# A two-layer model on one core: the first four rows' experts get blocks of their own, the last rows are routed beside them, and the state space's first fronts run beside the other blocks

## The chip, the cores and the metric

The kernel runs on one core of a Trainium2 chip. The core has TensorE (PE, matmuls; PEld is its weight load), VectorE (DVE), ScalarE (ACT), GpSimd (POOL) and SyncE (SP), a queue of DMA instructions for some of them, 16 DMA engines, and PSUM in eight banks of 128 x 512 float32. The time is device microseconds of one launch, the median of several runs. Everything is float32.

## The reference

The input x has 32 rows of 256 tokens of 128 numbers. There are two layers, each an attention-like part and a feed-forward part, and each part is wrapped in the same modulation, whose vectors come from one small matmul per layer:

```python
mod = (_silu(L0_c) @ L0_wmod).reshape(L0_c.shape[0], 6, 1, -1)
h = _layernorm(x, axis=-1) * (1 + ca) + sa
x = x + ga * _L0_attn_ref(h, ...)        # 16 heads of 8, rotary, softmax over 256 keys
h = _layernorm(x, axis=-1) * (1 + cb) + sb
x = x + gb * _L0_ffn_ref(h, ...)         # 8 experts, two per token
```

The feed-forward part of layer 0 gives every token its two best of eight experts:

```python
logits = x @ gate_w
mult, sel = _sparse_mixer_routing(logits)
w = jnp.sum(mult[:, :, None] * (sel[:, :, None] == jnp.arange(E)[None, None, :]), axis=1)
h = jax.nn.silu(jnp.einsum('th,ehf->etf', x, w1)) * jnp.einsum('th,ehf->etf', x, w3)
out = jnp.einsum('etf,efh,te->th', h, w2, w)
```

with 512 hidden units. Layer 1 replaces the attention by a Mamba-like state space in both directions (256 channels of 16 states, a scan over the 256 tokens) followed by a Fourier layer, and its experts take one expert per token with a capacity of 80. Only the path of layer 0's experts and the beginning of layer 1's state space matter here.

## The kernel before

**Attention (layer 0).** The order of the instructions is written out by hand. A loop runs over units `s`, eight to a row; a unit computes the scores of two heads of a row, `ex` (L572) and `q` (L576), with the weighted sums `weighted` beside them. Other work is cut into Python generators ("steps", each up to the next `yield`) and put between units: `prepared` (the next row's norm, rotary and projections), `turned` (transposes), `finished` (the output matmul L632, then y and x on POOL, L644 and L646).

**Routing.** `routed(first, n_rows, bank, apart)` (L314) takes a chunk of rows through its norm, gate logits, top two experts and the position of each token among the rows of its expert. `CHUNKS` cuts the 32 rows into six chunks of four and four chunks of two. A list `behind` holds the chunks under way; one step of the oldest is made per unit, two when more than one chunk is in it or in the last row. The last steps of a chunk are the scatters: per tile of 128 tokens two indirect DMAs on POOL's queue (`scattered`, L280; 16 for a chunk of four rows, 8 for one of two) write each token's row, with its destination and its multiplier, into the table `rows_in` in DRAM, in the expert's region. A counter `filled` (one number per expert) says how many rows an expert has so far. Before the first scatter the table has to be blank: `blanked` writes it in four DMAs of 8320 KB on ACT's queue in the units of rows 2 to 5.

**The joint.** The attention loop ends when all streams and `behind` are empty. Then rows 30 and 31 are routed (L781) with the instructions ordered by the compiler's own scheduler, which also schedules everything up to the state space. From `filled` VectorE computes the block table (L785 to L822): for each of `n_blocks` blocks which expert it belongs to, which rows it gathers (`at_u`) and which weights (`w_u`, which is set out of range where the buffer already holds that expert).

**Blocks.** `n_blocks` is 2 x 8192 / 256 + 8 - 1 = 71, since each expert's last block may be partly empty. A block (loop from L826) gathers its weights w (786,432 B, three buffers, L830) and 256 rows h (five buffers, L839) by indirect DMAs on POOL's queue, takes the destinations `to_u` out of h on VectorE (L847), transposes h on TensorE into the bank `ps_m` (L850, two buffers), copies hT (L852), multiplies by w1 and w3 (`pa`, `pb`, L861), gates with Silu on ACT (L862) and a product on VectorE (L863), multiplies by w2 (`po`, L869), scales on ACT (`o`, L877) and scatters the two halves into `rows_out` (L280). `weights_kept` (called at block 17) loads the state space's weights and computes from them `taps` (four POOL multiplies, L700), `spread_a`, `skip` and others.

**State space (layer 1).** Ordered by hand again: a loop over `g`, 16 units to a row, 512 in all, each with `arg` and `ub` matmuls (L1269), an exponential `da` (L1275), a product (L1286) and the scan (L1293) on VectorE, and a product with C on POOL (L1306). A row's unit can begin only when its `front` is done (L1005 to L1111): it adds the two expert outputs from `rows_out` to x, norms it twice, makes the in-projection, the convolution as matmuls, Silu, the x-projection, and dt and u through an exponential and a logarithm. A front is 22 steps, at the places `FRONT_AT` relative to the row's first unit, from -39 to -3.5; `gate` is one step at -9.5. For rows 0, 1 and 2 the loop starts at g = -39, so these steps have no units of another row beside them. A function `table` puts the loads of ACT's function tables where they are needed.

Of the kernel before, what the change touches and what calls it, by code (L numbers as in the profile page):

```python
# [69 lines left out]
def body(ctx: ExitStack, tc: tile.TileContext, a: dict, out: bass.AP):  # L70
# [155 lines left out]
    n_blocks = 2 * n_tok // BR + E - 1  # L226
# [11 lines left out]
    rows_out = scratch.tile([2 * n_tok, D], F32, tag="rows_out", name="rows_out")  # L238
    FILL = 16
    blank = rc.tile([P, FILL, WID], F32, tag="blank", name="blank")  # L240

    def blanked(part, parts):

        if part == 0:
            nc.gpsimd.memset(blank[:], 0.0)
            nc.gpsimd.memset(blank[:, :, D : D + 1], float(4 * n_tok))
        n = room // P // FILL // parts
        flat = rows_in[0:room, :].rearrange("(p a k) w -> p a (k w)", p=P, k=FILL)
        ins = nc.scalar.dma_start(
            flat[:, part * n : (part + 1) * n, :],  # L250
            blank[:].rearrange("p k w -> p (k w)").unsqueeze(1).to_broadcast([P, n, FILL * WID]),
        )
        blanks.append(ins.ins.name)
        if part == 0:
            nc.scalar.dma_start(rows_in[room:, :].rearrange("(p k) w -> p k w", k=2), blank[:, 0:2, :])
# [5 lines left out]
    nc.gpsimd.tensor_scalar(ids2[:], ids[:], float(n_tok), None, ALU.add)  # L261

    filled = rc.tile([P, E], F32, tag="filled", name="filled")
    nc.gpsimd.iota(
        filled[:], pattern=[[n_tok, E]], base=-1, channel_multiplier=0, allow_small_or_imprecise_dtypes=True
    )

    groups = {"in": [], "out": []}  # L270
    sync = mybir.DependencyInfo(mybir.DependencyClass.Sync, mybir.DependencyReason.DATA)
    blanks = []
# [3 lines left out]
    def scattered(group, apart=False, **args):  # L276

        if apart:
            nc.gpsimd.memset(spacer[:], 0.0)
        ins = nc.gpsimd.indirect_dma_start(in_offset=None, **args).ins  # L280
        tc.declare_no_dep(ins, group=group, reason="rows of their own")
        tc.add_to_no_dep_group(group, ins)
        for b in blanks if group == "in" else ():
            tc.add_manual_dep(ins, b, sync, reason="blank rows first")
        groups[group].append(ins.name)

    def reads(group, ins):
        for name in groups[group]:
            tc.add_manual_dep(ins.ins, name, sync, reason="scattered rows")

# [23 lines left out]
    def routed(first, n_rows, bank, apart):  # L314

        n = 2 * n_rows
        k = f"{n}_"
# [78 lines left out]
        for t in range(n):  # L396
            for row_u, h in zip(rows_at, hs):
                scattered(
                    "in",
                    apart,  # L400
                    out=rows_in[:],
# [4 lines left out]


    with ExitStack() as st:
# [8 lines left out]
        def a_bank():  # L417
            return ps_m.tile([P, 512], F32, tag="m", name="m")

# [231 lines left out]
        with tc.manual_schedule(engines=MANUAL):  # L651
            for s in range(-2 * UNITS_A - PREPARED, n_s + 9 * UNITS_A):
# [18 lines left out]
                if i == 2 and b - 2 in range(4):  # L671
                    blanked(b - 2, 4)
                last = b >= n_b - 1
                if i == (0 if last else 2) and b - 1 in starts[1:-1]:
                    c = starts.index(b - 1) - 1
                    behind.append(routed(starts[c], CHUNKS[c], a_bank, True))
                streams[:] = [w for w in streams if next(w, w) is not w]

                for _ in range(2 if last or len(behind) > 1 else 1):
                    if behind and next(behind[0], behind) is behind:  # L680
                        behind.pop(0)
                if s > n_s + UNITS_A + 1 and not streams and not behind:
# [7 lines left out]
    def weights_kept():  # L690
# [50 lines left out]


        das = [wc.tile([P, 4 * T + 1], F32, tag=f"da{i}", name=f"da{i}") for i in range(3)]
        for t in das:
            nc.gpsimd.memset(t[:, :: T], 0.0)

        behind = wc.tile([4 * DS, 1], F32, tag="behind", name="behind")
        nc.vector.tensor_copy(behind[:], ident[: 4 * DS, DTR : DTR + 1])
# [11 lines left out]


    with ExitStack() as st:
# [3 lines left out]
        ps_m = pool(st, "b_psm", 2, PSUM)  # L766
# [3 lines left out]
        iota_p = bc.tile([P, 1], F32, tag="iota_p", name="iota_p")  # L770
        nc.gpsimd.iota(iota_p[:], pattern=[[0, 1]], base=0, channel_multiplier=1, allow_small_or_imprecise_dtypes=True)
        iota_k = bc.tile([P, n_blocks], F32, tag="iota_k", name="iota_k")
        nc.gpsimd.iota(
            iota_k[:], pattern=[[1, n_blocks]], base=0, channel_multiplier=0, allow_small_or_imprecise_dtypes=True
        )
        empty = bc.tile([P, E], F32, tag="empty", name="empty")
        nc.gpsimd.iota(
            empty[:], pattern=[[n_tok, E]], base=-1, channel_multiplier=0, allow_small_or_imprecise_dtypes=True
        )

        for _ in routed(starts[-2], CHUNKS[-1], lambda: ps_m.tile([P, 512], F32, tag="m", name="m"), False):  # L781
            pass


        restart("k")  # L785
        blocks = thin(bc, E)
        nc.vector.tensor_tensor(blocks[:], filled[:], empty[:], ALU.subtract)
        nc.vector.tensor_scalar(blocks[:], blocks[:], 1.0 / BR, 0.5 - 0.5 / BR, ALU.mult, ALU.add)
        nc.vector.tensor_scalar(blocks[:], blocks[:], ROUND, None, ALU.add)
        nc.vector.tensor_scalar(blocks[:], blocks[:], -ROUND, None, ALU.add)  # L790
        upto = thin(bc, E)
        nc.vector.tensor_tensor_scan(upto[:], ones[:, :E], blocks[:], 0.0, ALU.mult, ALU.add)
        past = wide(bc, n_blocks)
        nc.vector.tensor_tensor(
            past[:],
            iota_k[:].unsqueeze(2).to_broadcast([P, n_blocks, E]),
            upto[:].unsqueeze(1).to_broadcast([P, n_blocks, E]),
            ALU.is_ge,
        )
        of = thin(bc, n_blocks)  # L800
        nc.vector.tensor_reduce(of[:], past[:], AX.X, ALU.add)
        nc.vector.tensor_tensor(past[:], past[:], blocks[:].unsqueeze(1).to_broadcast([P, n_blocks, E]), ALU.mult)
        at = thin(bc, n_blocks)
        nc.vector.tensor_reduce(at[:], past[:], AX.X, ALU.add)
        nc.vector.tensor_tensor(at[:], iota_k[:], at[:], ALU.subtract)
        nc.vector.tensor_scalar(at[:], at[:], float(P), None, ALU.mult)

        nc.vector.scalar_tensor_tensor(at[:], of[:], float(n_tok // 2), at[:], ALU.mult, ALU.add)
        nc.vector.tensor_scalar(at[:], at[:], float(room // 2), iota_p[:], ALU.min, ALU.add)
        at_u = bc.tile([P, n_blocks], U32, tag="at_u", name="at_u")  # L810
        nc.vector.tensor_copy(at_u[:], at[:])

        nc.vector.tensor_scalar(of[:], of[:], float(E - 1), float(P), ALU.min, ALU.mult)
        w_at = thin(bc, n_blocks)
        nc.vector.tensor_scalar(w_at[:], of[:], iota_p[:], None, ALU.add)
        same = thin(bc, n_blocks)
        nc.vector.tensor_tensor(same[:, WBUF:], of[:, WBUF:], of[:, : n_blocks - WBUF], ALU.is_equal)
        nc.vector.scalar_tensor_tensor(
            w_at[:, WBUF:], same[:, WBUF:], float(2 * E * P), w_at[:, WBUF:], ALU.mult, ALU.add
        )  # L820
        w_u = bc.tile([P, n_blocks], U32, tag="w_u", name="w_u")
        nc.vector.tensor_copy(w_u[:], w_at[:])  # L822

# [767 lines left out]
```

## Time and profile before

| what | us |
| --- | --- |
| median of the time | 3707.0 (3702.08 to 3708.46, three runs) |
| the profiled execution | 3705.42 |
| its span | 3703.6 |
| attention's last units | 840 to 862 |
| last scatter of rows 30 and 31 | 913.85 |
| first block's first pa | 924.77 |
| last po ends | 1334.9 |
| first arg of the state space | 1390.60 |
| first scan | 1396.33 |

The span is the profiled program from its first to its last instruction; the profiled execution's own time lies 1.8 us above it. "Busy" counts what an engine computes; POOL's time between two indirect DMAs is idle in these rows. A line of a timeline gives start, duration, engine, line, operation, output and inputs, and in brackets how long the engine was idle before and what released it. "PEclk" is the clock that TensorE was granted, as a share of full speed. The granted clock of the whole run was 0.897.

### The profile page before, as it was taken

The page shows a single profiled execution, that of the slowest core. Times are in us where ns is not written, and L with a number is a line of the kernel's source. Part 1 is how long each engine was busy: PE and PEld are TensorE (multiplying, and loading weights), DVE is VectorE, ACT ScalarE, POOL GpSimd, SP SyncE. Part 2 cuts the span into 40 slices and gives each one's busy share as a digit, 9 for nine tenths or more (in the row PEclk, how much of TensorE's full clock was granted, in tenths as well). Part 3 has the DMA queues.
Part 4 walks back from the last instruction along what each step waited for, and adds up shares of the span by engine and source line. Part 5 has one row for each costly group of instructions (what it writes and reads, how often), then busy time and mean ns, then how long its engine had stood idle before and what let it go on. Part 6 is the DMA issues. An engine that isn't in the chain of part 4 may idle for free. (4 is left out here: it accounts for less than half of the span.)

```text
span 3703.6 us, 69018 instructions
## 1 busy us (share of the span) xinstructions
PE 3147.8 (85%) x27464; PEld 2152.1 (58%) x27464; DVE 2612.1 (71%) x3526; ACT 2174.3 (59%) x3286; POOL 2683.4 (72%) x2724
## 2 busy tenths in 40 slices
PE   6988988883999968888889889889889889888864
PEld 3655655552888855555555555556556556555543
DVE  3566666653333318988888898888898888898952
ACT  2666666651333335667676676676676676577661
POOL 4465655555677747888888798888798887798852
PEclk6999999995999989898988898998898898899976
DMA  2630000002233311112112111111111111111112
GB/s 80 271 134 25 25 24 23 26 27 68 82 98 98 97 33 34 29 26 45 32 31 39 32 30 41 32 33 37 32 32 40 32 38 33 32 33 33 24 24 74
DMA packets 149688, 183.29 MB, mean 49 GB/s; under 512 B 31263, under 2 KB 112950, under 8 KB 145140
## 3 DMA queue, kind: packets, MB, share of 16 engines
q1 hardware_dynamic: 121892, 97.72, 11.6%
q0 software_dynamic: 23168, 46.93, 4.0%
q10 hardware_dynamic: 4304, 34.21, 2.2%
q8 instruction: 216, 3.54, 0.4%
q14 instruction: 108, 0.88, 0.1%
HBM read 130.24 MB, written 86.41 MB: 58 GB/s over the span
## 5 line engine op out<-in xcount | busy, mean ns | idle before, releaser
L1306 POOL TENSOR_TENSOR hs<-hs,bc 128x1024 f32<-128x1024 f32 x512 | 1207.0, 2367 | 302.2 <-DVE hs L1293 294.4
L1293 DVE TENSOR_TENSOR_SCAN hs<-da,ub 128x1024 f32<-128x1024 f32 x512 | 1166.1, 2277 | 30.9 <-DVE ub L1286 0.5
L1275 ACT ACTIVATE da<-arg 128x1020 f32<-128x1020 f32 x512 | 522.0, 1019 | 467.4 <-PE ub L1269 374.0
L1269 PE MATMUL arg<-dt,spread_a 32*128 32x256 f32 x4096 | 742.2, 434 | 40.2 <-ACT da L1275 39.2
L1269 PE MATMUL ub<-u,spread 32*128 32x256 f32 x4096 | 649.1, 437 | 88.3 <-POOL u L1111 46.6
L1286 DVE TENSOR_TENSOR ub<-ub,bc 128x1024 f32<-128x1024 f32 x512 | 620.7, 1212 | 40.8 <-PE ub L1269 40.5
L1269 PEld LDWEIGHTS arg<-dt,spread_a 32*128 32x128 f32 x4096 | 442.4, 200 | 201.8 <-ACT da L1275 84.0
L576 DVE TENSOR_REDUCE q<-x 128x4 f32<-128x1024 f32 x256 | 312.8, 1222 | 238.5 <-PE x L569 238.4
L1269 PEld LDWEIGHTS ub<-u,spread 32*128 32x128 f32 x4096 | 393.3, 203 | 143.3 <-DVE hs L1293 71.3
L572 ACT ACTIVATE ex<-e 128x1024 f32<-128x1024 f32 x256 | 262.1, 1024 | 204.6 <-PE x L569 193.5
L569 PE MATMUL e<-qmT,kqT 32*128 32x256 f32 x2048 | 340.9, 415 | 41.2 <-ACT ex L572 41.0
L1325 PE MATMUL y<-hs,gather 128*32 128x256 f32 x4096 | 344.5, 445 | 11.4 <-POOL hs L1306 11.3
L569 PE MATMUL x<-kqT 32*128 32x256 f32 x2048 | 306.8, 417 | 9.2 <-DVE q L576 9.2
L569 PEld LDWEIGHTS e<-qmT,kqT 32*128 32x128 f32 x2048 | 215.9, 191 | 100.2 <-ACT ex L572 72.6
L1053 PE MATMUL m<-oT,taps 128*128 128x256 f32 (+3 forms) x1024 | 264.0, 402 | 3.4 <-ACT xc L1056 2.0
L1180 PE MATMUL m<-coef,mag 128*128 128x128 f32 x1024 | 232.9, 313 | 38.8 <-DVE h L1188 29.1
L1053 PEld LDWEIGHTS m<-oT,taps 128*128 128x128 f32 x1024 | 190.2, 196 | 72.2 <-issue 37.9
L1325 PEld LDWEIGHTS y<-hs,gather 128*32 128x32 f32 x4096 | 123.9, 121 | 183.4 <-issue 98.4
L1180 PEld LDWEIGHTS m<-coef,mag 128*128 128x128 f32 x1024 | 173.8, 213 | 95.1 <-DVE h L1188 41.4
L1180 PE MATMUL m<-coef,r 128*128 128x128 f32 x1024 | 214.3, 294 | 0.0
L280 POOL DMA_INDIRECT rows_out<-o,to_u x142 | 144.5, 1018 | 87.5 <-ACT o L877 65.7
L569 PEld LDWEIGHTS x<-kqT 32*128 32x128 f32 x2048 | 187.6, 192 | 23.2 <-DVE q L576 19.8
(332 smaller groups left out, 6082.9 us busy)
## 6 DMA issues: line engine op xcount, KB each, us to landing
rows_in<-blank ACTq DMA_DIRECT2D x4, 8320.0 KB, 25.4
bc_d<-xd SPq DMA_DIRECT2D x64, 256.0 KB, 5.3
bc<-bc_d SPq DMA_DIRECT2D x32, 512.0 KB, 3.7
of_two<-rows_out SPq DMA_DIRECT2D x64, 128.0 KB, 2.6
mod_b<-mod SPq DMA_DIRECT2D x32, 256.0 KB, 4.0
mod<-mod SPq DMA_DIRECT2D x32, 192.0 KB, 3.1
x<-in_x SPq DMA_DIRECT2D x16, 256.0 KB, 5.3
mod<-mod SPq DMA_DIRECT2D x32, 128.0 KB, 3.0
```

Source lines behind the costliest of these rows:

```text
L280: ins = nc.gpsimd.indirect_dma_start(in_offset=None, **args).ins
L569: nc.tensor.matmul(to, lhs, rhs, start=True, stop=True)
L572: nc.scalar.activation(ex[:], exs[k_e][:], AF.Exp, scale=1.0 / math.sqrt(DH))
L576: nc.vector.tensor_reduce(pad("q", b)[:, :, 2 * i : 2 * i + 2, DH].rearrange("p t h -> p h t"), found[:], AX.X, ALU.max, negate=True,)
L1053: nc.tensor.matmul(to, taps[:, d, n, c, :], of, start=(s == 0), stop=(c == 0), skip_group_check=True)
L1180: nc.tensor.matmul(ps[:, t * D : (t + 1) * D], turned[k // (GRID // 2)][1 - j][:, k % (GRID // 2), t * P : (t + 1) * P], coef[:, j, k, :], ...
L1269: nc.tensor.matmul(to, lhs, rhs, start=True, stop=True)
L1275: nc.scalar.activation(e.da.rearrange("p (g t) -> p g t", t=T)[:, :, inner], e.arg[:].rearrange("p i j t -> p (i j) t")[:, :, inner], AF.Exp,)
L1286: nc.vector.tensor_tensor(by_four, by_four, b_of, ALU.mult)
L1293: nc.vector.tensor_tensor_scan(e.hs[:].rearrange("p g t -> p (g t)")[:, ::step], e.da[:, ::step], e.ub[:].rearrange("p i j t -> p (i j t)" ...
L1306: nc.gpsimd.tensor_tensor(e.hs[:], e.hs[:], c_of, ALU.mult)
L1325: nc.tensor.matmul(y[r * RG : (r + 1) * RG, :], gather[:, q, :], of.hs[:, 2 * j + p, :], start=False, stop=(q == NQ - 1), skip_group_check ...
```

## The change

Rows 0 to 3, chunk 0, get a table of their own (`early_in`, `early_out`), with counters of their own, and their block table is computed by VectorE during the attention, by two further steps put into `behind` after the routing of chunk 0 (so that chunk 0 is made at two steps per unit). Their 15 blocks (2 x 1024 / 256 + 7) come first; then 63 blocks for the other rows (2 x 7168 / 256 + 7), with the table computed after the last routing. `behind` is no longer advanced once the attention's units are over: what is left of rows 28 and 29, and the routing of rows 30 and 31, is made at two steps per early block. Beside the later blocks, from the 16th on, the steps of the first fronts for g = -39 to -3 are issued (all of row 0, 12 steps of row 1, three of row 2); the state space's loop then starts at g = -2. The state space's bank of PSUM lives through the blocks, and the blocks' transposes have one bank instead of two. `weights_kept` is called after the first later block; the buffers `das` are made in the state space itself; the blank tile and the chunk buffers of four rows live only in the attention.

```diff
-    n_blocks = 2 * n_tok // BR + E - 1
+    n_early = CHUNKS[0] * T
+    early_blocks = 2 * n_early // BR + E - 1
+    n_blocks = 2 * (n_tok - n_early) // BR + E - 1
...
+    early_in = scratch.tile([early_room + BR, WID], F32, tag="early_in", name="early_in")
+    early_out = scratch.tile([2 * n_early, D], F32, tag="early_out", name="early_out")
...
+    def early_table():
+        yield
+        early_at.append(block_table(rc, "j", early_blocks, early_filled, early_empty, n_early))
...
-    def routed(first, n_rows, bank, apart):
+    def routed(first, n_rows, bank, apart, rh, rt):
...
+        group, to_rows, filled = ("in", rows_in, later_filled) if first else ("early_in", early_in, early_filled)
...
-                if i == 2 and b - 2 in range(4):
-                    blanked(b - 2, 4)
+                if i == 2 and b - 2 in range(5):
+                    blanked(blank, b - 2, 4)
...
-                    behind.append(routed(starts[c], CHUNKS[c], a_bank, True))
+                    of_n = (wide_h, wide_t) if CHUNKS[c] > 2 else (rh, rt)
+                    behind.append(routed(starts[c], CHUNKS[c], routing_bank, True, *of_n))
+                    if c == 0:
+                        behind.append(early_table())
...
-                for _ in range(2 if last or len(behind) > 1 else 1):
+                for _ in range(0 if s >= n_s else 2 if last or len(behind) > 1 else 1):
                     if behind and next(behind[0], behind) is behind:
                         behind.pop(0)
-                if s > n_s + UNITS_A + 1 and not streams and not behind:
+                if s > n_s + UNITS_A + 1 and not streams:
                     break
...
+    ps_s = state_space.enter_context(tc.tile_pool(name="c_pss", bufs=1, space=PSUM, side="right"))
+    m_bank = ps_s.tile([P, 2 * T], F32, tag="m", name="m")
...
+        def step(self):
+
+            if self.at >= -2:
+                return False
+            self.begin(self.at)
+            self.steps(self.at)
+            self.steps(self.at + 0.5)
+            self.at += 1
+            return True
...
-        ps_m = pool(st, "b_psm", 2, PSUM)
+        ps_m = pool(st, "b_psm", 1, PSUM)
...
-        for _ in routed(starts[-2], CHUNKS[-1], lambda: ps_m.tile([P, 512], F32, tag="m", name="m"), False):
-            pass
...
-        for j in range(n_blocks):
-            if j == n_blocks // 4:
-                weights_kept()
...
+        behind.append(routed(starts[-2], CHUNKS[-1], routing_bank, False, rh, rt))
+        where = early_at[0]
+        for j in range(early_blocks):
+            block(j, where, "early_", early_in, early_out)
+            for _ in range(2):
+                if behind and next(behind[0], behind) is behind:
+                    behind.pop(0)
+        for steps in behind:
+            for _ in steps:
+                pass
+        where = block_table(bc, "k", n_blocks, later_filled, empty, n_tok)
+
+        for j in range(n_blocks):
+            block(j, where, "", rows_in, rows_out)
+            if j == 0:
+                weights_kept()
+            if j >= n_blocks // 4:
+                ahead.step()
+        while ahead.step():
+            pass
...
-            for g in range(FRONT_AT[0], n_u + 6 * UNITS):
+            fixed.append(True)
+            table(EXP_LN)
+            for g in range(ahead.at, n_u + 6 * UNITS):
+                ahead.begin(g)
```

`block_table` holds the operations of the table of before, and `block` those of a block, unchanged but for the tables they read and write; `front` and `gate` have moved out of the state space's loop, and their order of steps is that of before. `table` does nothing until `fixed` is set: beside the blocks the table loads are placed by the compiler.

## The prediction

> **What bounds the kernel now.** I read the stretches first, because the change touches only the attention's start, the expert blocks and the two joints around them. Columns: length, busy time of each engine, granted clock, DMA share, GB/s.
> ```profile
> core 0: us, PE busy (x) PEld busy (x) DVE busy (x) ACT busy (x) POOL busy (x), PEclk, DMA share, GB/s
> 886.00:925.00 39.00, 5.58 (x21) 4.26 (x22) 16.93 (x83) 5.08 (x11) 23.99 (x34) 0.50 0.40 125
> 935.00:1335.00 400.00, 397.30 (x2370) 349.02 (x2368) 130.14 (x275) 134.25 (x279) 275.96 (x274) 1.00 0.28 85
> 1335.00:1395.00 60.00, 27.48 (x100) 17.70 (x100) 3.52 (x21) 21.34 (x34) 21.84 (x36) 0.69 0.22 53
> 1395.00:1455.00 60.00, 50.90 (x422) 29.68 (x426) 56.18 (x43) 33.17 (x40) 45.00 (x28) 0.89 0.12 26
> ```
> TensorE bounds the blocks (397.30 of 400 us), VectorE the state space (56.18 of 60), and nothing is full in the 39 us before the blocks or the 60 us behind them: those are chains of single steps. Next, TensorE's instructions in the timeline, the blocks' first and last matmuls and the first state-space unit.
> ```profile
> 924.77 2.05 PE L861 MATMUL pa<-hT,w 128*128 128x256 f32 x4 [2.27 <-issue]
> ...
> 1314.19 0.61 PE L869 MATMUL po<-w,g 128*128 128x128 f32 x4
> 1314.63 0.60 PE L850 MATMUL m<-ident,h 128*128 128x128 f32 x4
> ...
> 1320.10 0.61 PE L869 MATMUL po<-w,g 128*128 128x128 f32 x4
> ...
> 1325.57 0.61 PE L869 MATMUL po<-w,g 128*128 128x128 f32 x4
> 1326.02 0.38 PE L850 MATMUL m<-ident,h 128*128 128x128 f32 x2
> 1326.59 0.71 PE L869 MATMUL po<-w,g 128*128 128x128 f32 x4 [0.19 <-DVE g L863]
> ...
> 1331.48 0.61 PE L869 MATMUL po<-w,g 128*128 128x128 f32 x4
> ...
> 1390.60 1.31 PE L1269 MATMUL arg<-dt,spread_a 32*128 32x256 f32 x8
> ```
> A block's first po stands at 1314.19, 1320.10, 1325.57, 1331.48: periods of 5.91, 5.47 and 5.91 us. Four transposes, for two blocks, sit behind the po at 1314.19; the next block has none, and pa of the block after it fills the wait for g. From the first po (931.41) to that of the last block, 70 periods, the mean is 5.715. The last pair, with two transposes a block, takes 5.91.
>
> POOL's groups from 940 to 1320 us, then two of the scatters (914 us) that end the last routing, with its taps:
> ```profile
> L280 POOL DMA_INDIRECT rows_out<-o,to_u x133 | 135.5, 1019 | 69.9 <-ACT o L877 48.5 <-issue 18.7 <-DVE to_u L847 1.5
> L830 POOL DMA_INDIRECT w<-in_moe,w_u x67 | 68.8, 1026 | 22.5 <-PE po L869 19.4 <-PE pa L861 2.5 <-PE pb L861 0.3
> L839 POOL DMA_INDIRECT h<-rows_in,at_u x65 | 63.0, 969 | 20.8 <-issue 19.5 <-DVE hT L852 1.3
> ```
> ```profile
> 893.29 4.95 POOL L700 TENSOR_TENSOR taps<-taps,in_w 128x512 f32<-128x512 f32 x4
> ...
> 912.58 0.96 POOL L280 DMA_INDIRECT rows_in<-h,4_row  x1 [0.30 <-DMA rows_in<-h,4_row]
> 913.85 0.96 POOL L280 DMA_INDIRECT rows_in<-h,4_row  x1 [0.30 <-DMA rows_in<-h,4_row]
> ```
> Each block issues four indirect DMAs on POOL: 2 x 1.02 + 1.03 + 0.97, with about 0.30 between them, 5.3 us of 5.715. POOL is the near second: 0.4 us of slack a block, 0.6 at 5.91. It reads 69% busy because the gaps don't count.
>
> The waits from 1335 to 1397 and from 200 to 280 us (total, times, longest):
> ```profile
> DVE st L296 <- POOL x L1020: 35.5, 3, 18.8
> ```
> ```profile
> POOL rows_in L280 <- DVE 8_w L389: 6.9, 1, 6.9
> ```
> The first is row 0's front alone on an empty chip; the second a four-row chunk routed beside the attention.
>
> **1. Earlier first block: -44 us.** The early blocks need only rows 0 to 3, so the 39 us of routing, scatters and table no longer stand ahead of them. What stays: the attention's last unit ends near 862, row 31's output matmul (L632) runs at about 874, its y and x on POOL by 876, then one w gather (1.03) and a landing. The h gathers go ahead, since their table is there. In before the first w was issued at 919.54 and pa followed at 924.77, 5.2 later, so the first pa falls at 881; 924.77 - 881 = 44. Ends: 878 (a landing of the median 2.2) and 888, -47 and -37.
>
> **2. Seven more blocks and one transposing bank: +55.** 15 early plus 63 late blocks replace 71. ps_m falls from two banks to one, because the state space's m bank lives through the blocks. With one bank, the transposes of a second block can't run ahead, and every block has the order of the last pair above: 5.91. From first po to last it was 70 x 5.715 = 400; it becomes 77 x 5.91 = 455. If the alternation survives, 77 x 5.715 = 440 (+40). Every early block loads its own weights (39 real loads instead of 24); I cost that at nothing, since w is gathered when its buffer of three is free, some 11 us ahead, and the slowest w landing in the stage was 5.7; the far end is one such landing, +5.7, where the lead is once lost.
> Here the trace prices the order at 5.91 against 5.47. The Trainium skill's "Perfetto Trace Analysis", section on optimizing matmuls, says that independent groups of matmuls should rotate through different PSUM banks, so that emptying one overlaps the next group: it speaks against this edit. By that rule this step is +55; had the second bank no worth, it would be +40.
>
> **3. Other TensorE work: +4.** Some 32 front matmuls (0.215 each at full clock; a group of eight took 1.96 at half clock) mostly fall into the wait of about 0.35 ahead of the second po group; I charge 0.09 each. The routing of the last rows adds 2.5, and the first blocks start a little sooner at full clock (-1.7). Ends +1 and +9.
>
> **4. POOL in the first early blocks: +11.** The scheduled order of the changed program puts here eight scatters left over from rows 28 and 29 (1.27 each), the four taps (4.95), the last routing's normed (1.8) and two h multiplies (2.4) are 19 us. POOL has 0.6 us a block and a lead: h is gathered about three blocks ahead. Over blocks 1 to 5 I let 8 us be absorbed: 19 - 8. Ends 0 (the lead takes all) and +19.
>
> **5. Eight scatters of rows 30 and 31: +9.** They stand in one run near block 9: 8 x 1.31 = 10.4. In the queue behind them wait the next w and h gathers and the scatters of the block just ended, so o's four buffers fill, ACT waits with o (L877), and TensorE follows. About 2 us of lead. Ends 0 and +10.4.
>
> **6. Fronts on POOL: +11.** Beside blocks 15 and later go all 22 steps of row 0's front, 12 of row 1's, 3 of row 2's. 13 multiplies of 0.72 + 0.08 and 5 normed of 1.45 are 17.7 us, most within blocks 16 to 21. Slack there is 6 x 0.6 = 3.6, and some 3 us go into gaps behind scatters. The transfers they need (landings 2.2 to 4.5) run on SP's queue, which the blocks leave empty. Ends 0 and +17.7.
>
> **7. The rest of the stage: +6.** The routing's Exp and row 0's Exp and Ln switch tables: the end of the trace of before shows loads of 1.28 (L992), some six in all, 7.7 us of which half hides. dt and u (2.35 each) hold POOL 4.7 us near block 46; with 2 to 3 us absorbed, two more each for ACT and POOL remain, and table k, some 8 us on VectorE beside blocks, costs 1. Ends +1 and +13.
>
> **8. The end of the stage: -55.** From the end of the last po (1334.9) to the first scan (1396.33) lie 61.4 us. Row 0's front is then ready; what remains is arg, da, ub and the scan's wait: 1396.33 - 1390.60 = 5.7, plus 0.7 for the das now cleared there. -55; ends -57 and -45 (a front that is late, or the loop's pools waiting for the blocks' last buffers).
>
> **9. Attention: +6.** Chunk 0 moves at two steps a unit: `early_table` stands behind it in `behind`. A chunk of four rows cost about 13 us in before: 25 units instead of 30 between 200 and 280 us. Packing the same 16 scatters and VectorE work into half the units raises the peak; the table adds about 4 us of VectorE. The blanks grow from 33.3 MB (4 x 8320 KB) by 4.26 MB, 10 us more at the 410 GB/s that the stretch 160 to 200 shows, beside which one mod row landed in 9.6 instead of 3 us and delayed POOL's h by 2.11. The wider pools, the moved blank tile and the iotas made earlier cost nothing: they change memory or run before the first row, where POOL is 40% busy; the iotas are 0.1 to 0.2 us each, below 1 us if they show. The two-row chunks at the end lose their two-step tail (leftovers go to blocks; counted above). Ends 0 and +13.
>
> **Sum.** -44 + 55 + 4 + 11 + 9 + 11 + 6 - 55 + 6 = +3. Steps 4 to 6 lean upward together, since each lag starts where the last has not been worked off (0.6 us a block), so I add 4: +7. The profiled execution took 3705.42 (span 3703.6), 1.6 below the median of 3707.0. 3705.4 + 7 = 3712.4, or 3714 against the median.
>
> **Rivals.**
> *A, POOL's queue eats both gains (forecast, 0.42):* 3700 to 3728. For it: 5.3 of 5.7 us of POOL are taken.
> *B, POOL's extra work hides (0.30):* if the gathers' lead absorbs most of the 31 us of steps 4 to 6, the result crosses no change once 24 are left (31 - 7). With 8 left: 3714 - 23 = 3691, faster than before. For it: 19.4 us of POOL's gaps ahead of w end with po, that is with TensorE, and h has up to three blocks of lead. Against: to_u (L847) waited 167.2 us for h in 66 waits, so the lead isn't slack everywhere.
> *C, the period stays at 5.7 (0.10):* if transposes are placed so that the one bank costs nothing, step 2 is +40: 3699. Against: 5.91 in the last pair, with exactly that order.
> *D, POOL keeps no lead (0.18):* everything put on POOL delays TensorE by its whole length, 19 + 10.4 + 17.7 = 47 instead of 31: 3714 + 16 = 3730, and 3737 where the attention also takes its upper end (+7). For it: the 0.30 us gaps, which POOL can't fill; against: the 48.5 us it waited for o.
>
> About 0.2% (7.4 us) is what a measurement of this kernel tells from no change: 3699.6 to 3714.4 counts as the same. Of A four tenths fall there, the rest above; of B five sixths below it, the rest within; half of C within, half below; D above. Faster 0.25 + 0.05 = 0.30, same 0.17 + 0.05 + 0.05 = 0.27, slower 0.25 + 0.18 = 0.43. The range, 3688 to 3740, takes in B's middle and all of D's; A alone is 3700 to 3728.
>
> **What would show it.** First pa near 881 (step 1). po to po 5.91 in undisturbed late blocks, with two transposes in each (2). Gaps of TensorE in the first five blocks, near block 9 and at late blocks 15 to 21, ended by h, w or o with POOL just behind (4 to 6). arg within about a microsecond of the last po and the first scan near 1403, 1396.33 + 7 (8). The attention's last unit at 862 plus 0 to 13 (9). Wrong would make it: POOL multiplies that don't delay a gather, a period under 5.8, a front that is late at the end, or an attention that loses more than 13 us.

## The result, and the profile after

The changed kernel takes 3727.1 us (3724.1 to 3733.0, five runs) against 3707.0 (3699.3 to 3709.1): a ratio of 1.0062, interval 1.0046 to 1.0077. It is slower, as forecast, but by 20 us, where the forecast was 7; 3727 lies at the upper end of rival A's own range. The profiled execution has a span of 3725.0 us, 21.4 more than before.

Cut at five points of the traces, the spans compare as follows (us; the last weighted sum is taken at its start, and the forecast is the sum of the prediction's steps for that stretch).

| stretch | before | after | difference | forecast |
| --- | --- | --- | --- | --- |
| start to the last weighted sum of the attention | 862.2 | 883.1 | +20.9 | +6 (step 9) |
| to the first pa | 62.5 | 18.2 | -44.3 | -44 (1) |
| to the end of the last po | 410.1 | 516.4 | +106.3 | +96, and 4 for the leaning (2 to 7) |
| to the first scan | 61.5 | 8.4 | -53.1 | -55 (8) |
| first scan to last scan | 2169.7 | 2167.8 | -1.9 | 0 |
| last scan to the end | 137.6 | 131.1 | -6.5 | 0 |

First the stretches of the profile after that answer to those shown of before (columns: length, busy time of each engine, clock, DMA share, GB/s).

```profile
core 0: us, PE busy (x) PEld busy (x) DVE busy (x) ACT busy (x) POOL busy (x), PEclk, DMA share, GB/s
884.00:901.00 17.00, 7.93 (x38) 4.85 (x30) 10.22 (x70) 2.74 (x6) 9.73 (x12) 0.60 0.29 90
930.00:1330.00 400.00, 367.29 (x2134) 322.16 (x2134) 129.85 (x325) 140.11 (x281) 276.69 (x293) 0.97 0.34 106
1418.00:1426.00 8.00, 3.71 (x32) 2.45 (x28) 1.20 (x1) 3.85 (x5) 1.15 (x4) 0.98 0.01 0
1426.00:1486.00 60.00, 53.30 (x446) 31.03 (x446) 56.20 (x44) 32.35 (x39) 46.00 (x31) 0.86 0.12 26
```

The joint of 39 us and more has shrunk to 17, the one of 60 to 8. TensorE, 397.30 of 400 us busy in the blocks before, now waits for 33 of 400. Next, TensorE's instructions in the timeline after: the last weighted sum, the first pa, two late blocks, and the seam to the state space.

```profile
883.12 1.94 PE L680 MATMUL o<-ex,v 128*32 128x256 f32 x16
...
901.34 2.08 PE L1079 MATMUL pa<-hT,w 128*128 128x256 f32 x4 [3.34 <-DMA w<-in_moe,w_u]
...
1372.94 0.61 PE L1087 MATMUL po<-w,g 128*128 128x128 f32 x4
1373.38 0.38 PE L1068 MATMUL m<-ident,h 128*128 128x128 f32 x2
1373.95 0.71 PE L1087 MATMUL po<-w,g 128*128 128x128 f32 x4 [0.18 <-DVE g L1081]
...
1378.85 0.61 PE L1087 MATMUL po<-w,g 128*128 128x128 f32 x4
...
1415.32 0.71 PE L1087 MATMUL po<-w,g 128*128 128x128 f32 x4 [0.41 <-DVE g L1081]
1415.97 0.70 PE L1366 MATMUL arg<-dt,spread_a 32*128 32x256 f32 x4
```

Each late block has its two transposes and lasts 1378.85 - 1372.94 = 5.91 us; arg starts even before the last po ends (1417.76). Both are as predicted. What was not: the attention ends 20.9 us later.

**Where the attention lost it.** Measured at the start of a unit's `ex`, units 0 to 44 (of 256) lie within 0.7 us of those of before. Between unit 45 (194 us) and unit 64 (279 us), while chunk 0 is routed, the kernel falls 26 us behind, 5 of which it gets back where before routed the end of its chunk. From row 9 on the distance stays at 20 to 22 us. This is one piece of the timeline of all engines after, at unit 46:

```profile
196.06 1.18 POOL L400 TENSOR_TENSOR h<-h,mod 128x512 f32<-128x512 f32 x1
197.32 1.18 POOL L401 TENSOR_TENSOR h<-h,mod 128x512 f32<-128x512 f32 x1
...
198.55 1.12 PE L157 MATMUL m<-ident,h 128*128 128x128 f32 x4 [3.84 <-POOL h L401]
...
199.70 0.59 ACT L406 COPY hT<-m 128x512 f32<-128x512 f32 x1 [3.81 <-PE m L157]
```

Two consecutive steps of `routed` stand in one unit: the products on POOL and the transposes that need them. TensorE reaches the transposes in its queue at once and stands there for 3.84 us, with the next unit's scores behind them; ACT waits as long. From 198 to 202 us, behind that wait, the granted clock is 0.50, and a matmul of the scores takes 0.63 us instead of 0.37. Two later waits of TensorE have other causes:

```profile
253.35 0.69 PE L614 MATMUL m<-ident,k 128*128 128x128 f32 x2 [5.76 <-POOL spacer L295]
...
265.06 0.78 PE L653 MATMUL x<-kqT 32*128 32x256 f32 x1 [3.17 <-DVE q L660]
```

The first and longest waits for k, whose rotary products on POOL stand behind eight of chunk 0's scatters in one run (241.2 to 251.0 us). The second waits for the reduction q, which stands on VectorE behind the whole early table (259.5 to 263.9 us), made in a single step.

**Where the blocks lost it.** Measured from a block's first o to the next, the blocks' distances are 5.91 except in six places and some single blocks (0.1 to 0.5 more). Over 5.91 each, blocks 2 to 6 took 10.8 us more, block 7 2.6, blocks 10 to 12 10.7, blocks 17 to 19 15.7, blocks 45 to 48 6.6, and blocks 34 to 44 some 3, where front matmuls fill more than the wait that each block has. Block 2 in the queues of four engines:

```profile
917.87 0.60 ACT L1080 ACTIVATE g<-pa 128x512 f32<-128x512 f32 x1 [0.93 <-PE pa L1079]
918.26 1.05 POOL L1057 DMA_INDIRECT h<-early_in,at_u  x1 [0.18 <-issue]
...
921.76 0.67 PE L1079 MATMUL pa<-hT,w 128*128 128x256 f32 x2 [2.62 <-DMA w<-in_moe,w_u]
922.05 2.57 DVE L1065 CAST to_u<-h 128x2 uint32<-128x2 f32 x1 [3.99 <-issue]
...
925.13 0.68 DVE L1081 TENSOR_TENSOR g<-g,pb 128x512 f32<-128x512 f32 x1
925.87 1.22 PE L1087 MATMUL po<-w,g 128*128 128x128 f32 x4 [3.44 <-DVE g L1081]
...
927.90 0.49 ACT L380 ACTIVATE h<-x,off,rstd 128x128 f32<-128x128 f32 x1 [9.43 <-POOL off L377]
928.30 0.35 ACT L1095 ACTIVATE o<-po,h 128x128 f32<-128x128 f32 x1
```

TensorE waits twice: 2.62 us for a w, whose gather POOL issued at 916.41 behind scatters of rows 28 and 29, and 3.44 us for the product g. The Silu for this g had run at 917.87, but on VectorE g stood behind a later block's to_u, whose h POOL gathered only at 918.26 and which landed at 921.97. The norm of the last routing (L380) waits 9.43 us on ACT for four small operations on POOL, which stand between taps, gathers and scatters; it delays the block's o, but TensorE's two waits don't end with it. In block 7 the last routing's gate matmuls, its chain on VectorE and four loads of ACT's function tables (1.28 us each) stand between the block's instructions. The waits of the changed kernel from 985 to 1000 us (block 11), and from 1046 to 1062 (blocks 18 and 19); columns are total, times, longest:

```profile
DVE to_u L1065 <- DMA h<-early_in,at_u: 7.4, 1, 7.4
PEld po L1087 <- DVE g L1081: 6.8, 1, 6.8
PE po L1087 <- DVE g L1081: 6.6, 1, 6.6
```
```profile
ACT o L380 <- POOL off L377: 7.1, 1, 7.1
PEld po L1087 <- DVE g L1081: 6.6, 2, 5.3
PE po L1087 <- DVE g L1081: 6.0, 2, 4.9
DVE st L368 <- POOL h L898: 4.0, 1, 4.0
```

At block 11 the eight scatters of rows 30 and 31 delayed the gathers of h; to_u waited for h on VectorE, and the product g, for which TensorE waits, stood behind it. At blocks 17 to 19 it is a front's norm that waits for POOL, and it holds two queues: TensorE's waits of 2.40, 1.11 and 1.11 us end with a Silu or an o that stood on ACT behind the norm's scale and offset (L380), those of 4.90 and 1.60 with a g that stood on VectorE behind the norm's statistics (L368), which waited for POOL's products.

### The profile page after: what moved, and what is told of

It is laid out like the page before. It is cut to its first block, busy times and chain, and to the rows that moved or that the text cites. A ratio compares the mean times of both kernels' runs of the same rounds, so it can differ in the third digit from the quotient of the medians.

```text
span 3725.0 us, 69770 instructions
## 1 busy us (share of the span) xinstructions
PE 3155.4 (85%) x27702; PEld 2168.2 (58%) x27702; DVE 2635.3 (71%) x3573; ACT 2190.6 (59%) x3319; POOL 2708.3 (73%) x2755
## 5 line engine op out<-in xcount | busy, mean ns | idle before, releaser
L1366 PE MATMUL arg<-dt,spread_a 32*128 32x256 f32 x4096 | 703.8, 423 | 57.1 <-ACT da L1372 56.1
L1366 PE MATMUL ub<-u,spread 32*128 32x256 f32 x4096 | 625.1, 423 | 80.4 <-POOL u L984 39.8
L1366 PEld LDWEIGHTS arg<-dt,spread_a 32*128 32x128 f32 x4096 | 421.8, 195 | 222.8 <-ACT da L1372 97.8
L1366 PEld LDWEIGHTS ub<-u,spread 32*128 32x128 f32 x4096 | 380.6, 196 | 123.9 <-DVE hs L1390 60.9
L1087 PE MATMUL po<-w,g 128*128 128x128 f32 x1248 | 189.2, 286 | 36.5 <-DVE g L1081 34.7
L1087 PEld LDWEIGHTS po<-w,g 128*128 128x128 f32 x1248 | 172.9, 196 | 66.5 <-DVE g L1081 51.9
## 6 DMA issues: line engine op xcount, KB each, us to landing
rows_in<-blank ACTq DMA_DIRECT2D x4, 8320.0 KB, 24.3
```

The source lines that it names most:

```text
L1087: nc.tensor.matmul(po[:, t * D : (t + 1) * D], g[:, c, t * P : (t + 1) * P], w[:, f : f + D], start=(c == 0), stop=(c == NF - 1), skip_gro ...
L1366: nc.tensor.matmul(to, lhs, rhs, start=True, stop=True)
```

## The experiments

### Chunk 0 at one step per unit

```diff
-                    behind.append(routed(starts[c], CHUNKS[c], routing_bank, True, *of_n))
-                    if c == 0:
-                        behind.append(early_table())
+                    work = routed(starts[c], CHUNKS[c], routing_bank, True, *of_n)
+                    behind.append(itertools.chain(work, early_table()) if c == 0 else work)
```

> The changed kernel with chunk 0 routed at one step per unit (its table still follows it); the blanks, the early blocks and all else stay. Theory 'pace': the 20.9 us that the attention lost come from two steps of one chunk in one unit, so that TensorE stands in its queue for a product that POOL has only just been given. Then the last weighted sum of the attention, at 883.1 in the changed kernel, falls to 863 to 868, and the time from 3727 to 3707 to 3712. Rival 'blanks': the 4.3 MB more of blank rows keep the DMA engines full for 10 us longer and the rows of mod late. Then the last weighted sum stays beyond 878 and the time beyond 3721.

Measured: 3710.7 us, ratio to the kernel before 1.0012 (1.0002 to 1.0022); the last weighted sum stands at 868.7, 14.4 us earlier than in the changed kernel. The stretch from 200 to 280 us, first of the changed kernel, then of this run:

```profile
200.00:280.00 80.00, 62.04 (x592) 38.99 (x588) 43.93 (x119) 36.54 (x67) 42.96 (x82) 0.85 0.47 183
```
```profile
200.00:280.00 80.00, 70.71 (x770) 47.08 (x767) 50.55 (x118) 48.34 (x88) 51.72 (x98) 0.96 0.50 196
```

At one step per unit TensorE makes 770 instead of 592 matmuls in these 80 us, at a granted clock of 0.96 instead of 0.85, under the same blank rows. The pace is the cause of 14 of the 21 us; how they divide between the product put directly ahead of its transposes and the run of scatters was not told apart. The trace of this run shows where the remaining 6.5 (868.7 against 862.2) come from:

```profile
279.78 0.29 DVE L319 TENSOR_TENSOR jt<-early_filled,early_empty 128x8 f32<-128x8 f32 x1
...
285.22 0.17 DVE L354 CAST w_u<-jt 128x15 uint32<-128x15 f32 x1
285.30 1.22 DVE L660 TENSOR_REDUCE q<-x 128x4 f32<-128x1024 f32 x1
...
286.57 0.79 PE L653 MATMUL x<-kqT 32*128 32x256 f32 x1 [4.04 <-DVE q L660]
```

Up to unit 72 it lies 1 to 2.4 us behind the kernel before, and it doesn't fall back further while the longer blanks are written. In units 73 and 74, where the whole early table stands on VectorE ahead of q for 5.5 us, it loses 6.3 us.

### Two transposing banks, one po bank

```diff
-        ps_m = pool(st, "b_psm", 1, PSUM)
+        ps_m = pool(st, "b_psm", 2, PSUM)
-        ps_o = pool(st, "b_pso", 2, PSUM)
+        ps_o = pool(st, "b_pso", 1, PSUM)
```

> The changed kernel with two PSUM banks for the blocks' transposes again, paid for by one bank instead of two for po. Theory 'alternation': undisturbed pairs of blocks take 5.91 + 5.48 again, up to 77 x 0.2 = 15 us less from the first po to the last, 3712 to 3717; stalls where POOL is late grow a little, since a shorter block leaves POOL 0.4 instead of 0.6 us. Rival 'POOL's pace': POOL's four DMAs of 5.3 us and the added work set the stage's length, so the time stays within 4 us of 3727. A third: a single po bank makes the next po wait for ACT, and the time rises.

Measured: 3722.1 us, ratio 1.0046 (1.0030 to 1.0061), between the two theories. The trace separates them: from block 0 to block 49 the stage takes 319.9 us instead of 339.5, with the pairs of 5.48 and 5.91; from there to block 77 it takes 190.4 instead of 167.3. Up to block 49 the two banks are worth 20 us, of which the shorter pairs explain about half (49 x 0.215 = 10.5), and something later takes 23 away (the last experiments look for it). The third theory has a part: before block 49, 12.4 us of TensorE's waits end with ACT's o, against 1.5 in the changed kernel. POOL's pace is not what sets 5.91.

### The kernel before with one transposing bank

```diff
-        ps_m = pool(st, "b_psm", 2, PSUM)
+        ps_m = pool(st, "b_psm", 1, PSUM)
```

> The kernel before with one PSUM bank for the blocks' transposes, nothing else. Theory 'alternation': every block takes 5.91, so 70 x (5.91 - 5.715) = 14 us more: 3721. Rival: the order doesn't matter, since the saved wait comes back elsewhere: within 4 us of 3707.

Measured: every undisturbed block takes 5.91 us, and the stretch from the first pa to the last po 423.2 instead of 410.1: 13.1 more, where 14 was expected. The time is 3713.0, ratio 1.0017 (1.0007 to 1.0027), only 6 us more, between the two theories. The profiled execution is at the upper end of its runs; the period decides for the alternation, and where the times get the other 7 us back was not found.

### No front steps beside the blocks, in two ways

```diff
-            if j >= n_blocks // 4:
-                ahead.step()
-        while ahead.step():
-            pass
```

> The changed kernel with no front steps beside the blocks; the state space's loop starts at its step -39 again. My steps 6 to 8: the stalls at late blocks 17 to 19 (15.6 us over 5.91 a block) and most of the 12 us over it in the remaining blocks go, and the gap between the last po and the first scan grows from 8.4 to about 61: 3727 + 53 - 25 = 3755, 3748 to 3762. Rival: the fronts cost the blocks nothing and those stalls have another cause: 3780.

Measured: 3720.8 us, and the first scan still follows the last po by 8.9 us. Both theories missed. The fronts stand beside the blocks here too: row 0's first product is on POOL at 1027.1. Without the calls the fronts come later in the program, but that is not their place in the queues: row 0's front needs only `early_out`, its pool and its bank exist during the blocks, and the scheduler moves what is ready forward. What lets the fronts start early is then not the loop that issues the steps, but, as argued here, the separate table and the bank. The second way therefore makes the loads wait:

```diff
-            reads(group, nc.sync.dma_start(of_two[:, i], of_i.rearrange("(t p) d -> p t d", p=P)))
+            ins = nc.sync.dma_start(of_two[:, i], of_i.rearrange("(t p) d -> p t d", p=P))
+            reads(group, ins)
+            reads("out", ins)
```

> The changed kernel with no front step issued beside the blocks, and each front's two loads made to wait for all scatters of the late blocks too, so that the scheduler can't move them forward as it did in the run without front steps. If that run's result came from the scheduler moving the fronts by itself, the last po now follows the first pa by 516 - 26 = 490 us (485 to 495), the first scan follows the last po by 55 to 65 instead of 8.4, and the time is 3727 + 53 - 26 = 3754 (3746 to 3760). Rival: fronts were never what lengthened the stage; then it stays near 514 and the time is 3775 or more.

Measured: 3756.1 us, ratio 1.0134 (1.0118 to 1.0151); 491.7 us from the first pa to the last po, 64.5 to the first scan, as expected. Blocks 17 to 19 take 5.91, 5.91 and 6.19. The fronts beside the blocks cost them 516.4 - 491.7 = 25 us and save 56 behind them.

### The fronts' products on VectorE

```diff
+    def by():
+        return nc.gpsimd if fixed else nc.vector
...
-        nc.gpsimd.tensor_tensor(of_two[:, 0], of_two[:, 0], of_two[:, 1], ALU.add)
+        by().tensor_tensor(of_two[:, 0], of_two[:, 0], of_two[:, 1], ALU.add)
```

and so for the front's other six products and sums.

> The changed kernel with the fronts' products and sums beside the blocks (13 of 128x256, and dt and u of row 0) on VectorE instead of POOL; the norms' small operations stay on POOL. Theory 'POOL's queue': the blocks from 17 to 19 took 8.1 + 10.5 + 14.8 us instead of 17.7 because products stood between the gathers and scatters of POOL's queue. Then these three fall to under 22 together, the pair near block 46 by some 4 us, and the time from 3727 to 3708 to 3716. Rival: they wait for the fronts' transfers or for the norms, on whichever engine the products stand; then the three stay above 28, and the time within 5 us of 3727.

Measured: 3711.8 us, ratio 1.0016 (1.0006 to 1.0025); the stage is 502.3 us. Blocks 17 to 19 take 10.0 + 7.4 + 5.9 = 23.3 instead of 33.4, blocks 45 to 48 24.3 instead of 30.2. The three are a little over the 22 that was expected, and the waits from 1030 to 1060 us say why:

```profile
PEld po L1090 <- DVE g L1084: 6.3, 6, 1.6
ACT o L1098 <- PE po L1090: 5.8, 4, 3.0
ACT o L380 <- POOL off L377: 5.6, 2, 4.6
PE po L1090 <- DVE g L1084: 4.6, 5, 1.3
```

The norms' small operations are still on POOL and ACT still waits for them, 4.6 us at most instead of 7.1. Blocks 16 and 20 now take 7.0 and 7.4, so that of the 10 us saved in blocks 17 to 19 some 7 are left.

### Pace, products, taps and scatters together, with one bank and with two

To the pace of chunk 0 and the fronts' products on VectorE come these:

```diff
-                nc.gpsimd.tensor_tensor(
+                nc.vector.tensor_tensor(
                     taps[:, d, n],
...
-            nc.gpsimd.tensor_tensor(tiles(h, 2), tiles(h, 2), per_row(mod, CB - SB, 2), ALU.mult)
+            eng = nc.gpsimd if apart else nc.vector
+            eng.tensor_tensor(tiles(h, 2), tiles(h, 2), per_row(mod, CB - SB, 2), ALU.mult)
...
-            for _ in range(2):
+            for _ in range(2 if j < 8 else 1):
```

> The changed kernel with chunk 0 at one step per unit, the fronts' products on VectorE, also the taps and the last routing's two products on VectorE, and the last scatters of rows 30 and 31 made one pair per block instead of in one run. Theory: the three causes add up: 16 us from the attention, 13 from the fronts, 5 to 12 from the early blocks: 3727 - 37 = 3690 (3683 to 3698), faster than the kernel before. Rival: once POOL is relieved another engine's queue (VectorE, which now holds the taps in front of g) takes the place, and no more than 20 us come together: 3705 or more.

Measured: 3688.2 us (3685.6 to 3693.1), ratio 0.9956 (0.9942 to 0.9970): faster than both kernels, and within 2 us of the sum of the parts. The stage takes 496.5 us, the attention ends at 869.8. Not all of the three causes are gone:

```profile
963.00 0.98 POOL L1060 DMA_INDIRECT h<-early_in,at_u  x1 [0.30 <-issue]
...
983.93 0.98 POOL L1060 DMA_INDIRECT h<-rows_in,at_u  x1 [0.31 <-issue]
...
986.90 0.17 DVE L1068 CAST to_u<-h 128x2 uint32<-128x2 f32 x1 [8.21 <-DMA h<-rows_in,at_u]
...
989.14 1.22 PE L1090 MATMUL po<-w,g 128*128 128x128 f32 x4 [5.67 <-DVE g L1084]
```

The steps were halved, but on POOL the last eight scatters still stand within 14 us (966 to 980), with no gather of h between 963.0 and 983.9. Blocks 10 to 14 take 10.1 us over 5.91 each, where the changed kernel took 11.2. So the gain comes from the attention and the products, and that of spread scatters was not measured.

> The same with two PSUM banks for the transposes and one for po. Theory: with POOL relieved, the shorter pairs of blocks of the run with two banks keep their 15 to 20 us: 3670 to 3680. Rival: at 5.7 us a block POOL's 5.3 leave no room for what is still on it (the norms, the scatters of the last rows), and the gain is under 6 us over the one bank.

Measured: 3698.6 us, ratio 0.9977 (0.9968 to 0.9987): 10 us slower than with one bank, though its undisturbed pairs are the short ones. The theory fails, and the rival has the sign but not the reason: from 1199 to 1338 us TensorE is busy for 133.91 of 139 us, so it is not POOL that holds it. From block 49 to block 67, ten blocks take 6.8 to 12.9 us. TensorE's timeline there:

```profile
1245.12 0.60 PE L929 MATMUL m<-oT,taps 128*128 128x255 f32 x2
...
1246.23 1.02 PE L929 MATMUL m<-oT,taps 128*128 128x254 f32 x4
...
1247.98 0.60 PE L1071 MATMUL m<-ident,h 128*128 128x128 f32 x4
...
1248.91 0.65 PE L945 MATMUL m<-xc,xp 128*64 128x256 f32 x2 [0.32 <-ACT xc L935]
```

and in the run with one bank, where a block's transposes and a front's matmuls share the wait for g:

```profile
1147.21 0.61 PE L1090 MATMUL po<-w,g 128*128 128x128 f32 x4
1147.66 0.38 PE L1071 MATMUL m<-ident,h 128*128 128x128 f32 x2
1147.97 0.65 PE L945 MATMUL m<-xc,xp 128*64 128x256 f32 x2
1148.55 0.71 PE L1090 MATMUL po<-w,g 128*128 128x128 f32 x4
```

With two banks pa of the next block fills that wait, nothing is free, and the fronts' matmuls lengthen the blocks in full: 62 of them from block 49 to 67, 18 us of TensorE, while the excess over 5.695 a block (the mean of 5.48 and 5.91) is 24.5 there. With one bank the same fronts raise some ten blocks by 0.3 to 0.4 us. The bank and the front matmuls fill the same hole. Two other things differ. With one bank the scheduler set the front matmuls two to a block, in blocks 18 to 52; with two it set them from block 47 on, up to ten in a block, and an even order with two banks was not tried. And po has one bank instead of two, but from block 49 to 67 no wait of TensorE ends with ACT's o.

### to_u behind g

One block of the last run took 12.85 us: VectorE held two copies hT behind a to_u that waited 3.85 us for a late h. So to_u was tied behind the block's last product:

```diff
-            nc.vector.tensor_copy(to_u[:], h[:, :, D])
...
+            ins = nc.vector.tensor_copy(to_u[:], h[:, :, D])
+            tc.add_manual_dep(ins.ins, last.ins.name, sync, reason="after g")
```

> The version with all causes removed and one transposing bank (3688), and to_u taken from h only after the block's last product g on VectorE. With one bank the undisturbed period is set by TensorE at 5.91, so both theories leave it: 3688 less at most 6, for the few blocks where to_u held VectorE while h was late.

> The version with two transposing banks and one po bank (3698.5), and to_u taken from h only after the block's last product g. Theory 'queue': the alternation of 5.48 and 5.91 pays, and the long blocks from 51 to 68 came from to_u of a later block, waiting on VectorE for an h that landed late, ahead of the copies hT that TensorE needs. With to_u behind g those blocks fall to under 6.5, and the time to 3668 to 3680. Rival 'lead': h itself lands too late because POOL has no room at 5.7 us a block, so the long blocks stay, under another name, and the time stays at 3692 or more.

> The kernel before with to_u taken from h only after the block's last product g, nothing else. VectorE waited 167 us for h in to_u, but TensorE was busy for 397 of 400 us there: within 4 us of 3706 by either theory. Were it faster by more, to_u would have been a cost of its own in the kernel before, and no part of the comparison.

These three ran on another chip, where the kernel before itself takes 3742.2 us, so only their ratios say something, and not the microseconds expected. With one bank: 0.9911 (0.9896 to 0.9927). With two: 0.9958 (0.9945 to 0.9972). The kernel before with the edit: 0.9985 (0.9975 to 0.9994), 5 us. In the second the block of 12.85 falls to 5.96, and the other long ones stay (7.8, 7.5, 8.7, 8.3 and 8.6): to_u was the cause of that one block, and the front matmuls, 60 of them from block 49 to 67, are the likely one of the rest. Two banks are again the slower choice. Whether the first is better than the same version without the edit (0.9956 on the first chip) can't be told across two chips. On this chip the short pairs don't hold: the kernel before with the edit shows periods of 5.48 and mostly 6.8, and the version with one bank its 5.91. Why a block is longer there when its transposes alternate was not found; no trace of the unedited kernel on that chip exists.

## Why the prediction was right, and where it was off

The direction and the range held, and the steps on the two joints and the period were right to 2 us. The attention lost 15 us more than forecast and the blocks 6 more, and 8 us that no step had came back behind the first scan; without this luck the time would have been some 3735, still in the range but above that of rival A. By its steps:

- **Step 1** (-44) measured -44.3. The chain was read correctly: row 31's last matmul, y, one w and its landing (x came behind the w). The attention's later end only shifted it.
- **Step 2** (+55) held: 5.91 in every undisturbed late block, and the lost bank alone costs the kernel before 13.1 us in the stage (6 in the times) where the step implied 14. The second half of the argument, that the bank is a pure loss, failed: beside front matmuls, in the order that the scheduler made here, the second bank is worth nothing, because they fill the same wait. The rule of the Trainium skill that was weighed there ("Perfetto Trace Analysis", Optimizing Tensor Performance: rotate independent groups through different PSUM banks) agrees with the kernel before (13.1 us in the stage) and not with the changed one with its fronts (10 us the other way, with one bank for po).
- **Step 4** (+11) measured 10.8 over 5.91 in blocks 2 to 6: a w and an h gathered late, as forecast. **Step 5** (+9) measured 10.7, but not by the path given: o's four buffers did not fill; to_u on VectorE waited for h, ahead of g. **Step 6** (+11) was too small: 15.7 at blocks 17 to 19, since a late POOL doesn't only delay gathers but holds the queues of VectorE and ACT through the norm's statistics and its scale and offset, ahead of g and Silu. With the products off POOL 10 of these 15.7 us go, and 2.7 come back in the blocks beside them. **Steps 3 and 7** (+4 and +6) came to about 14 together: 10 in blocks 34 to 48, 2.6 in block 7, the rest in single blocks. Step 3 counted 32 front matmuls of 0.215 us; the trace has 68, two in each of 34 blocks, and most fit the wait. (The group of eight in 1.96 us that it read as half clock ran at a granted clock of 1.00.) All in all 106 instead of 100.
- **Step 8** (-55) measured -53.1, with arg before the last po's end. By the run with late fronts it is worth 56 against 25 in the blocks: by far the best part of the change.
- **Step 9** (+6) is the step that failed: +20.9. It named the doubled pace and the table, but priced what they add to the engines, and not what they hold up: two steps in one unit put the transposes directly behind their product, and chunk 0's scatters ahead of k's rotary products, and the table in one step stands ahead of q, each in queues that can't pass it. Its upper end, 13, left that out too. At one step per unit 6.5 remain, and 6.3 are lost where the table stands; the longer blanks show no cost there.
- **The end**: no step had the 6.5 us between the last scan and the end. All ten traced versions of the changed kernel have 131 to 134 us there, the kernel before 137.5 and 137.6 with one bank and with two (140.0 with to_u moved, on the other chip). The clock granted in the last stretches is 0.81 from 3680 to 3704 us before and 0.93 from 3702 to 3726 after; why full speed comes sooner stays open.

Rival A was the case in the blocks (37 us for steps 4 to 6, where it had 31), at its upper end by the attention; B fell, since POOL's lead hid little; D is near in size for another reason, the attention.

## What to carry to other kernels

When work is woven by hand between the units of a pipeline, price the distance between a step and the one that consumes it, and what stands behind each in its queue, not only their durations: doubling the pace of one chunk cost 14 us here with no instruction added, and a table of 5.5 us in one step 6.3. Before giving two uses the same slack (a wait for g, a queue's 0.4 us), count who fills it already: the second PSUM bank is worth 13 us of the stage alone, and was worth less than nothing here once other matmuls stood in the hole. And a small operation that a busy queue delays costs what stands behind its consumer: here a to_u of 0.17 us that waited for a late h held g, and with it TensorE, for 6.59 us, and a front's norm that waited for POOL's products held it for 4.90.

## What the runs showed of the hardware that was not expected

TensorE's granted clock fell to 0.85 over the 80 us in which the attention waited (0.96 at one step per unit); in the 4 us behind the wait of 3.84 us it was 0.50, so a wait also slowed the matmuls behind it. The small cast to_u on VectorE, 0.17 us in most blocks, took 2.57 and 1.78 us where the taps' products ran on POOL, and ended with them (924.62 and 924.59, 932.98 and 932.89); in the run with the taps on VectorE and one bank none took over 0.42 us. The kernel before was 1% slower on one chip (3742 against 3707), and there the blocks with alternating transposes had periods of 5.48 and 6.8 us, where those with one bank kept 5.91.
